# Four graph-attention layers on one core: alternating the step order to its end, and a new path for the last step

## The chip, the cores and the metric

The kernel runs on one core of a Trainium2 chip. TensorE (PE) does matrix products and transposes, VectorE (DVE), ScalarE (ACT) and GpSimd (POOL) do elementwise work, and SyncE (SP) issues the DMAs. Each engine works through its own instructions in program order; where one needs another's result it waits on a semaphore. The metric is device microseconds of one execution, the median of several; lower is better. All times below are microseconds unless marked ns.

## The reference

Sixteen independent batches of 1,024 nodes with 256 features go through four graph-attention layers. Each layer normalises its input, projects it, weighs every pair of neighbouring nodes and adds the weighted sum to its input:

```
h  = relu(layernorm(x))
q  = h @ W                      # heads: 4, 1, 4, 1
e  = leaky_relu(src(q)[i] + dst(q)[j])     # slope 0.2, 0.2, 0.2, 0.01
a  = softmax over j of e, where adj[i, j]
x += elu(a @ q)                 # relu in the last layer
```

`src` and `dst` are scalar products of a head's features with two halves of a vector. All is float32.

## The kernel before

**Steps.** A step is one layer of one batch: 64 steps. Layers 0 and 2 have four heads of 64 features (a *four-head* step), layers 1 and 3 one head of 256 (a *one-head* step). A batch's layers depend on each other, so four streams of batches are interleaved; `order_of_steps` (L635) lists the stream of each step in `turns`. The order alternates four-head and one-head steps, but its last nine entries end in four-head, four-head, one-head, one-head, one-head (steps 59 to 63: batches 14, 15, 13, 14, 15; layers 2, 2, 3, 3, 3). The last step, 63, is the last layer of batch 15; step 60 is the layer before it.

**The sum of a step.** The weight of a pair is written as a maximum of two products, so that for a head and a block of 128 nodes `jc` one VectorE instruction makes a tile of 128 x 1,024 unnormalised weights (`weights`, L386-391): the larger of `g` (a row spread over all partitions, in PSUM) and `rcol` (a column), times the 0/1 mask. There are 8 tiles per head, 32 in a four-head step. `aggregate` (L393) multiplies the tiles on TensorE with the projected features `whx` (L405), in eight groups a step, k = 0 to 7. A four-head group is half a head's nodes, a one-head group one block of 128 nodes over all 8 tiles. An extra column gives the sum of the weights, by which `finish` divides. ScalarE copies a group's sums from PSUM to `y` (L420). The tiles live in 18 buffers (`WBUFS`), so VectorE can be at most 18 tiles ahead of TensorE. Group sums, projections and transposes share four PSUM banks (`bank`).

**Finishing a step.** `finish(n)` (L426) returns pieces, each with the group of step n + 1 behind which it is emitted: the reciprocal of the sums (`divide`, L441, VectorE); `scaled` per half of the nodes: on VectorE min(y, 0) times the reciprocal (L451, layers with ELU and slack), on GpSimd y times the reciprocal (L452); the exponential on ScalarE (L458); and `add`: on VectorE max(exp - 1, y) (L464), on GpSimd the addition to x (L465). In the last layer, which has relu, `add` is one VectorE instruction (L467), and `store` writes the result out.

**Preparing a step.** `preparation(n)` (L229) returns 21 pieces in a fixed order: `stats` of two halves (four `bn_stats` each, L241), the combination of the moments, on VectorE for step 0 and else on GpSimd (L268-280; the power -0.5 is GpSimd's always, L274), `normalise` of two halves (ScalarE, L286), then per half two pieces of `transpose` and four of `project`, then `factors`, `rows`, the fetch of the heads, and an end mark. From step 2 on, the transpose goes through ScalarE (L295), a DMA transpose and ScalarE again (L303). Steps 0 and 1 transpose on TensorE (L317) and copy on ScalarE (L318). `project` is 4 matmuls a block (L328), a copy (L330), and at the end of a half two exponentials on ScalarE and a multiplication of `whx` on GpSimd (L340). `rows` transposes the factors (L352) and stores them in DRAM; `fetch` loads them spread over the partitions, and `broadcast` copies them to PSUM (`g`, ScalarE, L384). Only head 0 of step 0 makes `g` by eight TensorE transposes (L381).

**The order around it.** Everything is emitted by hand. Each kind of step has a table of 21 due times (`FOUR`, `ONE`, `NEXT`, `TIGHT` and others), counted in groups, eight to a step, from a start two steps ahead of its own. The main loop emits, for each group: tiles it still needs, the group's matmuls, pieces of `finish` that are due, heads, prepared pieces that are due, and tiles ahead. In the last step each group's division, relu, addition and store follow at once on VectorE and SP (L414-417).

Of the kernel before, what the change touches and what calls it, by code (L numbers as in the profile page):

```python
# [26 lines left out]
F32 = mybir.dt.float32  # L27
# [5 lines left out]
ALU = mybir.AluOpType  # L33
# [3 lines left out]
P = 128  # L37
# [3 lines left out]
WBUFS = 18  # L41
HBUFS = 6
# [4 lines left out]

FOUR = (-8, -8, -5, 0, 1, 0, 3, 5, 5, 5, 5, 1, 4, 5, 5, 5, 5, 6, 8, 8, 10)  # L50
SHORT = (-4, -4, -4, 0, 1, 0, 3, 5, 5, 5, 5, 1, 4, 5, 5, 5, 5, 6, 8, 8, 10)
NEXT = (-4, -4, -4, 1, 3, 2, 5, 8, 8, 8, 8, 4, 7, 8, 8, 8, 8, 9, 10, 10, 12)
# [1 line left out]
SOON = (0, 0, 0, 1, 2, 1, 3, 4, 4, 5, 5, 2, 5, 6, 6, 7, 7, 7, 8, 8, 10)  # L54
FIRST = (-4, -4, -4, -2, -0.9, -1, -1, -0.8, -0.8, -0.8, -0.8, 0, 0, 1, 1, 1, 1, 1, 2, 2, 4)
TIGHT = (4, 4, 4, 5, 6, 5, 7, 8, 8, 8, 8, 6, 8, 9, 9, 9, 9, 9, 10, 10, 12)
LATE = (0, 0, 0, 1, 2, 1, 3, 4, 4, 4, 4, 2, 4, 5, 5, 5, 5, 5, 6, 6, 8)


# [9 lines left out]
def kernel(ctx: ExitStack, tc: tile.TileContext, x, adj, ws, avs, out):  # L69
    nc = tc.nc  # L70
    B, N, F = x.shape
    C = N // P
# [156 lines left out]
    def preparation(n):  # L229
# [6 lines left out]
        def stats(half):  # L236
            if half == 0:
                st["bn"] = small.tile([P, C, 6], F32, name="bn")
            bn = st["bn"]
            for c in range(half * HALF, (half + 1) * HALF):  # L240
                nc.vector.bn_stats(bn[:, c, :], xs[b][:, c, :])  # L241
            q = slice(half * HALF, (half + 1) * HALF)
            if n == 0:
                if half == 1:
                    combine_end(slice(0, HALF), nc.vector)
                combine(q, nc.vector)
            elif H == 1:

                combine(q, nc.gpsimd)
                combine_end(q, nc.gpsimd)  # L250
# [55 lines left out]
                st["turned", half].rearrange("p s n i -> p (n i) s"), AF.Copy)  # L306

        def transpose(half, k):
            if n > 1:

                (merge if k else split)(half)
                return
            if k == 0:
                st["hT", half] = prep.tile([P, K, HALF * P], F32, name="rows", bufs=HBUFS)
            pt = bank(HALF, P)
            for q in range(HALF):
                nc.tensor.transpose(pt[:, q, :], st["xn", half][:, k, q, :], ident)  # L317
            nc.scalar.activation(st["hT", half][:, k, :], pt.rearrange("p q i -> p (q i)"),  # L318
                                 AF.Copy)
# [28 lines left out]

        def rows():

            pt = bank(P)[0:C * H]
            nc.tensor.transpose(pt, st["gcol"].rearrange("p c h -> p (c h)"), ident)  # L352
            gT = small.tile([C * H, P], F32, name="gT", bufs=2)
            nc.scalar.activation(gT, pt, AF.Copy)
            st["grow"] = dram.tile([H, C, P], F32, name="grow")
            nc.sync.dma_start(out=st["grow"].rearrange("h c i -> c h i"), in_=gT)
# [5 lines left out]


        out += [factors, rows, lambda: fetch_heads(n + 1), lambda: None]
        return [(at, piece) for at, piece in zip(agenda_of[n], out, strict=True)]

    def fetch(n, h):

        if n == 0 and h == 0:
            return  # L370
        gs = state[n]["gs", h] = work.tile([P, N], F32, name="gs", bufs=2)
        nc.sync.dma_start(out=gs, in_=state[n]["grow"][h].rearrange("c i -> (c i)")
                          .partition_broadcast(P))

    def broadcast(n, h):

        g = state[n]["g", h] = ps_g.tile([P, N], F32, name="g")
        if n == 0 and h == 0:

            for c in range(C):  # L380
                nc.tensor.transpose(g[:, c * P:(c + 1) * P],  # L381
                                    state[n]["gcol"][:, c, h:h + 1].to_broadcast([P, P]), ident)
            return
        nc.scalar.activation(g, state[n]["gs", h], AF.Copy)  # L384

    def weights(n, h, jc):  # L386

        w = state[n]["w", h, jc] = work.tile([P, N], F32, name="w", bufs=WBUFS)
        nc.vector.scalar_tensor_tensor(w, state[n]["g", h], state[n]["rcol"][:, jc, h:h + 1],  # L389
                                       masks[LAYERS[steps[n][1]][3]][:, jc, :],  # L390
                                       op0=ALU.max, op1=ALU.mult)

    def aggregate(n, h, i0, per):  # L393
        H = LAYERS[steps[n][1]][0]
# [31 lines left out]
    def finish(n):  # L426

        b, l = steps[n]
        H = LAYERS[l][0]
        D = F // H  # L430
        st = state[n]

        def views(half):
            s = slice(half * HALF, (half + 1) * HALF)
            return (xs[b][:, s, :].rearrange("p c (h d) -> p (c h) d", h=H),
                    st["y"][:, s, :, 0:D].rearrange("p c h d -> p (c h) d"),
                    st["r"][:, s, :].rearrange("p c h -> p (c h)"))

        def divide():
            st["r"] = small.tile([P, C, H], F32, name="r")  # L440
            nc.vector.reciprocal(st["r"], st["y"][:, :, :, D])  # L441

        def scaled(half):
            xh, yh, r = views(half)
            rb = r[:, :, None].to_broadcast([P, HALF * H, D])
            if l < L - 1:

                e = st["e", half] = prep.tile([P, HALF * H, D], F32, name="rows",
                                                    bufs=HBUFS)
                if H > 1 and slack(n):  # L450
                    nc.vector.scalar_tensor_tensor(e, yh, 0.0, rb, op0=ALU.min, op1=ALU.mult)  # L451
            nc.gpsimd.tensor_tensor(yh, yh, rb, op=ALU.mult)  # L452
            if l < L - 1 and not (H > 1 and slack(n)):
                nc.gpsimd.tensor_scalar(e, yh, 0.0, -3.0e38, op0=ALU.min, op1=ALU.max)  # L454

        def exponential(half):
            if l < L - 1:
                nc.scalar.activation(st["e", half], st["e", half], AF.Exp)  # L458

        def add(half):  # L460
            xh, yh, r = views(half)
            if l < L - 1:
                e = st["e", half]
                nc.vector.scalar_tensor_tensor(e, e, -1.0, yh, op0=ALU.add, op1=ALU.max)  # L464
                nc.gpsimd.tensor_add(xh, xh, e)  # L465
                return
            nc.vector.scalar_tensor_tensor(xh, yh, 0.0, xh, op0=ALU.max, op1=ALU.add)  # L467

        def store(half):
            nc.sync.dma_start(  # L470
                out=out[b].rearrange("(p c) f -> p c f", p=P)[:, half * HALF:(half + 1) * HALF],
                in_=xs[b][:, half * HALF:(half + 1) * HALF, :])
            if half == 1 and b + STREAMS < B:
                load(b + STREAMS)


        at = (0, 0, 0, 0, 1, 1, 1) if slack(n) and H > 1 else (0, 0, 1, 1, 2, 2, 3)
        return list(zip(at, (divide, lambda: scaled(0), lambda: scaled(1), lambda: exponential(0),
                             lambda: exponential(1), lambda: add(0), lambda: add(1)))) + (
                    [(4, lambda: store(0)), (4, lambda: store(1))] if l == L - 1 else [])  # L480
# [60 lines left out]
    for n, (b, l) in enumerate(steps):  # L541

        free = -99
        if b % STREAMS in last:
            over = last[b % STREAMS] + 1
            free = 8 * over + (8 if l == 0 else 2 if LAYERS[steps[over][1]][0] == 1 else 4)
        last[b % STREAMS] = n
        start = 8 * (n - 2)
        kind = ONE if LAYERS[l][0] == 1 else SOON if n < 3 else FOUR
        if kind is FOUR and free > start + kind[0]:  # L550
            kind = SHORT if slack(n - 2) else NEXT
        if kind is ONE and free > start + kind[0]:
            kind = TIGHT
        if free > start + kind[0]:
            kind = LATE
            start = max(free, agenda_of[-1][0] + 5, start - LATE[7])
        agenda_of.append([start + k for k in kind] if n > 1 else FIRST)
        if n > 2:


            assert agenda_of[n][7] >= 8 * (n - 2)
            assert agenda_of[n][3] >= agenda_of[n - 1][12]
    ending = []
    later = {}
    with tc.manual_schedule():
# [45 lines left out]
        for n in range(len(steps)):  # L611
            for k, (h, i0, per) in enumerate(groups(n)):
                while planned < len(steps) and min(
                        a[0] for a in agenda_of[planned:planned + 2]) <= 8 * n + k:
                    plan(planned)
                    planned += 1
                emit_tiles(place[n, h, C - 1] + 1, must=True)
                aggregate(n, h, i0, per)
                if i0 + per == C:
# [15 lines left out]
def order_of_steps(B, L):  # L635

    depth = B // STREAMS * L
    one = [[(k // L * STREAMS + s, k % L) for k in range(depth)] for s in range(STREAMS)]  # L640
    turns = [0, 1, 2, 0, 3, 1, 2] + [0, 3, 1, 0, 2, 1, 3, 2] * (depth // 2 - 2)
    turns += [0, 3, 1, 0, 2, 3, 1, 2, 3]
    return [one[s].pop(0) for s in turns]


# [22 lines left out]
```

## Time and profile before

| | |
|---|---|
| median of 3 runs | 2460.33 (2455.75 to 2462.64) |
| the profiled execution's own time | 2463.54 |
| its span, first to last instruction | 2461.8 |
| granted TensorE clock, mean | 0.994 |
| weights, VectorE L389 | 1,280 instructions, 1,273 ns mean, 1538.9 busy |
| sums, TensorE L405 | 36,864 instructions, 240 ns mean, 1899.5 busy |
| projections, TensorE L328 | 2,048 instructions, 393 ns mean, 489.3 busy |
| chain of waits by engine | PE 82%, ACT 6%, DVE 5%, DMA 4%, issue 2% |
| last matmul ends, us from the start | 2457.7 |

A row of the profile names the line, the engine, the operation, the tile written and the tiles read, then their shapes and a count. In the view in order of time the first two numbers are the start and the length of the row; several like instructions in a row are merged, and `[5.55 <-PE bank L405]` says that the engine had been idle for 5.55 us and what released it. Since a matmul's end is modelled and overlaps the next one, lengths of matmuls are best read from one row's start to the next row's start.

### The profile page before, as it was taken

Reading aid. Unit: us, or ns where it says so; the run is one execution under the profiler, and the core shown is the slowest. Engines: PE = TensorE matmul, PEld = TensorE weight load, DVE = VectorE, ACT = ScalarE, POOL = GpSimd, SP = SyncE. Lnnn points to the kernel's source line nnn. Section 1 sums busy time; section 2 is a strip of 40 time slices with the busy share of each in tenths; the row PEclk is TensorE's granted clock in tenths of the full one; section 3 lists DMA queues with packets and bytes.
Section 4 is the critical chain, followed back from the end, with each engine's and each line's share of the span. In section 5 each row is a group of like instructions: output and inputs, shape, how many; then the busy total and the mean of one; then the engine's idle time right before and its main releaser. Section 6 shows DMA issues by size and latency. Waiting matters only on the chain.

```text
span 2461.8 us, 86525 instructions
## 1 busy us (share of the span) xinstructions
PE 2396.4 (97%) x39104; PEld 2150.2 (87%) x39104; DVE 2041.2 (83%) x2138; ACT 1484.9 (60%) x2501; POOL 1074.7 (44%) x1366
## 2 busy tenths in 40 slices
PE   7989999999999999999999999999999999999899
PEld 5888798889898889898898888899988889888878
DVE  8988688888888988888988888988888888888963
ACT  5464676555666656765556765656665556765461
POOL 3344455543345454444343555453444344553341
PEclk9999999999999999999999999999999999999999
DMA  4322232233333322232433332323433422323221
GB/s 181 81 54 62 44 79 62 70 105 90 94 85 87 74 64 56 67 79 88 113 97 81 77 71 62 79 63 80 113 79 87 109 58 54 79 62 70 77 48 61
DMA packets 294761, 193.40 MB, mean 79 GB/s; under 512 B 264182, under 2 KB 266998, under 8 KB 292472
## 3 DMA queue, kind: packets, MB, share of 16 engines
q1 hardware_dynamic: 294382, 187.86, 30.2%
q8 instruction: 306, 5.01, 0.8%
q14 instruction: 63, 0.52, 0.1%
q10 hardware_dynamic: 10, 0.00, 0.0%
HBM read 105.39 MB, written 17.43 MB: 50 GB/s over the span
## 4 chain that ended last, share of the span: by engine, by line
PE 82%; ACT 6%; DVE 5%; DMA 4%; issue 2%; POOL 0%; SPq 0%; DVEq 0%; ACTq 0%
PE bank L405 64%; PE bank L328 18%; DVE w L389 4%; ACT rows L286 2%; DMA gs<-grow 2%; DMA grow<-gT 1%; ACT rows L295 1%; ACT g L384 1%; ACT rows L458 1%; ACT rows L303 1%; DVE bn L241 1%; ACT y L420 0%; DMA rows<-rows 0%; PE bank L352 0%; DVE rows L464 0%
## 5 line engine op out<-in xcount | busy, mean ns | idle before, releaser
L405 PE MATMUL bank<-whx,w 128*64 128x65 f32 x36864 | 1899.5, 240 | 26.4 <-DVE w L389 17.0
L405 PEld LDWEIGHTS bank<-whx,w 128*64 128x64 f32 x36864 | 1746.2, 144 | 186.5 <-issue 22.6
L389 DVE SCALAR_TENSOR_TENSOR w<-g,rcol,mask 128x1024 f32<-128x1024 f32 x1280 | 1538.9, 1273 | 206.1 <-PE bank L405 160.8
L340 POOL TENSOR_TENSOR whx<-whx 128x1024 f32<-128x1024 f32 x128 | 244.9, 1913 | 823.8 <-ACT whx L338 823.8
L420 ACT ACTIVATE y<-bank 128x260 f32<-128x260 f32 (+1 forms) x504 | 191.9, 381 | 567.1 <-PE bank L405 567.0
L328 PE MATMUL bank<-wx,rows 128*128 128x264 f32 (+1 forms) x2048 | 489.3, 393 | 16.0 <-ACT y L420 8.4
L328 PEld LDWEIGHTS bank<-wx,rows 128*128 128x128 f32 x2048 | 384.4, 192 | 92.5 <-ACT y L420 14.2
L452 POOL TENSOR_TENSOR y<-y,r 128x1024 f32<-128x1024 f32 x126 | 262.4, 2091 | 254.0 <-DVE rows L451 186.6
L330 ACT ACTIVATE whx<-bank 128x264 f32<-128x264 f32 (+1 forms) x512 | 193.6, 388 | 194.2 <-PE bank L328 193.5
L286 ACT ACTIVATE rows<-x,shift,rstd 128x256 f32<-128x256 f32 x512 | 264.5, 588 | 72.5 <-POOL shift L280 70.3
L465 POOL TENSOR_TENSOR x<-x,rows 128x1024 f32<-128x1024 f32 x96 | 227.1, 2365 | 181.6 <-DVE rows L464 181.6
L303 ACT ACTIVATE rows<-rows 128x2048 uint16<-128x2048 uint16 x124 | 265.9, 2144 | 21.5 <-DMA rows<-rows 21.5
L295 ACT ACTIVATE rows<-rows 128x2048 uint16<-128x2048 uint16 x124 | 236.9, 1911 | 3.9
L464 DVE SCALAR_TENSOR_TENSOR rows<-rows,y 128x1024 f32<-128x1024 f32 x96 | 187.9, 1957 | 49.1 <-ACT rows L458 43.7
L241 DVE BATCH_NORM_STATS2 bn<-x 128x6 f32<-128x256 f32 x512 | 175.5, 409 | 33.4 <-POOL x L465 30.0
L384 ACT ACTIVATE g<-gs 128x1024 f32<-128x1024 f32 x159 | 162.6, 1023 | 63.8 <-DMA gs<-grow 49.1
L274 POOL TENSOR_TENSOR rstd<-rstd,neghalf 128x4 f32<-128x4 f32 (+1 forms) x97 | 120.3, 1240 | 15.2 <-DVE shift L275 7.8
L458 ACT ACTIVATE rows<-rows 128x1024 f32<-128x1024 f32 x96 | 100.6, 1048 | 2.0 <-POOL rows L454 2.0
L441 DVE RECIPROCAL r<-y 128x32 f32<-128x32 f32 (+1 forms) x63 | 17.2, 274 | 96.3 <-ACT y L420 96.3
L451 DVE SCALAR_TENSOR_TENSOR rows<-y,r 128x1024 f32<-128x1024 f32 x58 | 70.1, 1250 | 1.1
L467 DVE SCALAR_TENSOR_TENSOR x<-y,x 128x1024 f32<-128x1024 f32 x30 | 36.5, 1215 | 8.9 <-POOL y L452 8.9
L338 ACT ACTIVATE whx<-whx,nbias 128x16 f32<-128x16 f32 (+1 forms) x128 | 40.3, 315 | 4.2
(67 smaller groups left out, 444.4 us busy)
## 6 DMA issues: line engine op xcount, KB each, us to landing
gs<-grow SPq DMA_DIRECT2D x159, 512.0 KB
x<-in_x SPq DMA_DIRECT2D x15, 1024.0 KB
out<-x SPq DMA_DIRECT2D x30, 512.0 KB
w<-in_adj SPq DMA_DIRECT2D x8, 512.0 KB
rows<-rows SPq DMA_TRANSPOSE x124
x<-in_x SPq DMA_DIRECT2D x2, 512.0 KB
wx<-in_L_gnn_W SPq DMA_DIRECT2D x8, 128.0 KB
out<-x SPq DMA_DIRECT2D x8, 128.0 KB
```

The lines of the kernel that those rows point to most:

```text
L241: nc.vector.bn_stats(bn[:, c, :], xs[b][:, c, :])
L286: nc.scalar.activation(xn[:, :, q, :], xs[b][:, c, :].rearrange("p (k i) -> p k i", k=K), AF.Relu, bias=st["shift"][:, c:c + 1], scale=st[ ...
L295: nc.scalar.activation(bits, xn.rearrange("p (n s) -> p s n", s=2), AF.Copy)
L303: nc.scalar.activation(st["hT", half].rearrange("p k i -> p (k i)").bitcast(U16).rearrange("p (n s) -> p n s", s=2), st["turned", half].re ...
L328: nc.tensor.matmul(pw, lhsT=st["hT", half][:, k, q * P:(q + 1) * P], rhs=wx[l][:, k, :], start=(k == 0), stop=(k == K - 1))
L330: nc.scalar.activation(st["whx"][:, c, :], pw, AF.Copy)
L340: nc.gpsimd.tensor_tensor(wh[:, :, :, 0:D], wh[:, :, :, 0:D], wh[:, :, :, D:D + 1].to_broadcast([P, HALF, H, D]), op=ALU.mult)
L389: nc.vector.scalar_tensor_tensor(w, state[n]["g", h], state[n]["rcol"][:, jc, h:h + 1], masks[LAYERS[steps[n][1]][3]][:, jc, :], op0=ALU.m ...
L405: nc.tensor.matmul(acc[o % P:o % P + cols, q, :], lhsT=st["w", h, jc][:, o:o + cols], rhs=st["whx"][:, jc, h * (D + 1):(h + 1) * (D + 1)], ...
L420: nc.scalar.activation(st["y"][:, i0:i0 + per, h, :], acc, AF.Copy)
L452: nc.gpsimd.tensor_tensor(yh, yh, rb, op=ALU.mult)
L465: nc.gpsimd.tensor_add(xh, xh, e)
```

## The change

The last nine entries of `turns` are replaced by one more round of the regular eight and a final stream 3. So steps 60 and 61 change places: 60 is batch 13's last layer (one head), 61 batch 15's third (four heads), then 62 and 63 as before. Only step 62 now stands between a step and the last one, which needs its result.

- The last step is prepared by a table of its own, `LAST`, which starts at step 62. Its three statistics pieces do nothing; `finish` of step 61 calls them through `state[-1]`.
- `finish` of step 61 consists of `begin` (emitted before step 62's first group), the exponential of half 1, and `end` (both behind group k = 1). All of it is VectorE's but the two exponentials. The statistics of step 63 stand between its pieces, combined on VectorE.
- Step 63's transposes go by TensorE, its `rows` are left out, and its `g` is made by eight TensorE transposes (`direct`).
- Step 63's weights are made in two halves of 512 columns, the first half of all eight tiles first.
- Step 60's `add` is two GpSimd instructions instead of one of VectorE.

```diff
+LAST = (0, 0, 0, 1, 3, 2.8, 2.8, 4, 4, 4, 4, 4, 4, 4, 4, 4, 4, 4, 5, 5, 5)
...
-            if n == 0:
+            if n == len(steps) - 1:
+                combine(q, nc.vector)
+            elif n == 0:
...
-            if n > 1:
+            if 1 < n < len(steps) - 1:
...
+            if n == len(steps) - 1:
+                return
             pt = bank(P)[0:C * H]
...
+        if n == len(steps) - 1:
+            st["stats"], st["combined"] = stats, lambda half: combine_end(
+                slice(half * HALF, (half + 1) * HALF), nc.vector)
+            out[0:3] = [lambda: None] * 3
...
+    def direct(n, h):
+
+        return h == 0 and n in (0, len(steps) - 1)
...
+        parts = 2 if n == len(steps) - 1 else 1
+        if parts > 1 and jc:
+            return
+        js = range(C) if parts > 1 else (jc,)
+        for j in js:
+            state[n]["w", h, j] = work.tile([P, N], F32, name="w", bufs=WBUFS)
+        for i in range(parts):
+            s = slice(i * N // parts, (i + 1) * N // parts)
+            for j in js:
+                nc.vector.scalar_tensor_tensor(
+                    state[n]["w", h, j][:, s], state[n]["g", h][:, s],
+                    state[n]["rcol"][:, j, h:h + 1],
+                    masks[LAYERS[steps[n][1]][3]][:, j, s], op0=ALU.max, op1=ALU.mult)
...
+            if n == len(steps) - 4:
+
+                nc.gpsimd.tensor_scalar(yh, yh, 0.0, 3.0e38, op0=ALU.max, op1=ALU.min)
+                nc.gpsimd.tensor_add(xh, xh, yh)
+                return
...
+        if n == len(steps) - 3:
+
+            def early(half):
+                xh, yh, r = views(half)
+                rb = r[:, :, None].to_broadcast([P, HALF * H, D])
+                e = st["e", half] = prep.tile([P, HALF * H, D], F32, name="rows", bufs=HBUFS)
+                nc.vector.scalar_tensor_tensor(e, yh, 0.0, rb, op0=ALU.min, op1=ALU.mult)
+                if half == 0:
+                    exponential(half)
+                nc.vector.tensor_tensor(yh, yh, rb, op=ALU.mult)
+
+            def late(half):
+                xh, yh, r = views(half)
+                e = st["e", half]
+                nc.vector.scalar_tensor_tensor(e, e, -1.0, yh, op0=ALU.add, op1=ALU.max)
+                nc.vector.tensor_add(xh, xh, e)
+
+            def begin():
+                divide()
+                early(0)
+                late(0)
+                state[-1]["stats"](0)
+                early(1)
+                state[-1]["combined"](0)
+
+            def end():
+                late(1)
+                state[-1]["stats"](1)
+                state[-1]["combined"](1)
+
+            return [(-1, begin), (1, lambda: exponential(1)), (1, end)]
...
+        if n == len(steps) - 1:
+            kind, start = LAST, 8 * (n - 1)
...
+                while ending and ending[0][0] < k:
+                    ending.pop(0)[1]()
                 emit_tiles(place[n, h, C - 1] + 1, must=True)
...
-    turns = [0, 1, 2, 0, 3, 1, 2] + [0, 3, 1, 0, 2, 1, 3, 2] * (depth // 2 - 2)
-    turns += [0, 3, 1, 0, 2, 3, 1, 2, 3]
+    turns = [0, 1, 2, 0, 3, 1, 2] + [0, 3, 1, 0, 2, 1, 3, 2] * (depth // 2 - 1) + [3]
```

More of the change, by code (lines that the diff above doesn't have):

```diff
@@ L364, in preparation @@
         out += [factors, rows, lambda: fetch_heads(n + 1), lambda: None]
+        if n == len(steps) - 1:
+            st["stats"], st["combined"] = stats, lambda half: combine_end(
+                slice(half * HALF, (half + 1) * HALF), nc.vector)
+            out[0:3] = [lambda: None] * 3
         return [(at, piece) for at, piece in zip(agenda_of[n], out, strict=True)]
+    def direct(n, h):
+        return h == 0 and n in (0, len(steps) - 1)
     def fetch(n, h):
-        if n == 0 and h == 0:
+        if direct(n, h):
             return
@@ L377, in broadcast @@
         g = state[n]["g", h] = ps_g.tile([P, N], F32, name="g")
-        if n == 0 and h == 0:
+        if direct(n, h):
             for c in range(C):
@@ L386, in weights @@
     def weights(n, h, jc):
[L388 to L391, printed above, removed]
+        parts = 2 if n == len(steps) - 1 else 1
[11 more added lines that the diff above has]
+                    masks[LAYERS[steps[n][1]][3]][:, j, s], op0=ALU.max, op1=ALU.mult)
     def aggregate(n, h, i0, per):
```

## The prediction

> **What bounds the kernel now.** I read the page's busy shares first, then the busy time by stretch, then TensorE alone in order of time.
>
> ```profile
> PE 2396.4 (97%) x39104; PEld 2150.2 (87%) x39104; DVE 2041.2 (83%) x2138; ACT 1484.9 (60%) x2501; POOL 1074.7 (44%) x1366
> ```
>
> TensorE is the bound: only its idle time can be won. The next view cuts the end of the run into two ordinary pairs of a four-head and a one-head step (55-56, 57-58) and everything after step 58. Columns: stretch, its length, busy us of PE, PEld, DVE, ACT, POOL, granted clock, DMA share, GB/s.
>
> ```profile
> 2117.80:2192.20 74.40, 74.01 (x1220) 66.45 (x1219) 63.02 (x65) 47.21 (x80) 36.62 (x44) 1.00 0.28 66
> 2192.20:2266.40 74.20, 73.55 (x1219) 66.19 (x1218) 62.27 (x58) 48.33 (x81) 30.93 (x24) 1.00 0.31 70
> 2266.40:2457.80 191.40, 179.26 (x2565) 158.92 (x2564) 124.54 (x140) 80.37 (x142) 64.35 (x84) 0.98 0.21 59
> ```
>
> Where the steps alternate, TensorE idles 0.4 to 0.7 us per pair. In the last five steps it idles 12.1 us, and the clock is not whole. The waits of TensorE in this last stretch name the cause (us, times, longest):
>
> ```profile
> PE bank L405 <- DVE w L389: 6.2, 9, 0.9
> PE bank L405 <- issue: 3.1, 4, 1.2
> PE bank L328 <- ACT rows L303: 2.6, 1, 2.6
> ```
>
> Steps 59 and 60 are both four-head, and 64 tiles of weights at 1.20 us make VectorE late. The rows of TensorE give the price of its work:
>
> ```profile
> 2323.47 11.42 PE L405 MATMUL bank<-whx,w 128*64 128x65 f32 x384
> ...
> 2361.25 5.75 PE L328 MATMUL bank<-wx,rows 128*128 128x258 f32 x16 [2.62 <-ACT rows L303]
> ...
> 2415.74 41.98 PE L405 MATMUL bank<-whx,w 128*128 128x257 f32 x192
> ```
>
> 384 matmuls to the next start take 11.35 us, so a four-head step (1,024) takes 30.3 us; 192 take 41.8, so a one-head step (128) takes 27.9; half a projection undisturbed is 3.67 us, a whole one 7.35. Work after step 58: 2 x 30.3 + 3 x 27.9 + 4 x 7.35 + 0.4 for four row transposes = 174.1 us. The stretch is 191.3, so **17.2 us are lost**: 12 as idle, 2.1 because the 16 matmuls above took 5.75 instead of 3.67, the rest in matmuls drawn out between late tiles.
>
> **The change, part by part.** Nothing differs before the preparations of steps 60 and 61, around 2230 us; I rebuild the time from 2266.4 on.
>
> *Steps 59 and 60* become one more ordinary pair: 74.3 us, the mean of the two above.
>
> *Step 61* (four-head, batch 15) keeps the one-head preparation for step 62, but loses the 7.35 us projection of a four-head step two ahead. Step 57 is its model: from 2192.2 to 2238.4, 46.2 us. Its 32 projection matmuls with a wait held 8.2 us (2222.53 to 2230.77). Step 61: 46.2 - 8.2 = 38.0. That projection was also VectorE's cover:
>
> ```profile
> 2206.53 7.24 DVE L389 SCALAR_TENSOR_TENSOR w<-g,rcol,mask 128x1024 f32<-128x1024 f32 x6 [5.55 <-PE bank L405]
> ...
> 2228.16 9.61 DVE L389 SCALAR_TENSOR_TENSOR w<-g,rcol,mask 128x1024 f32<-128x1024 f32 x8
> 2238.92 0.35 DVE L441 RECIPROCAL r<-y 128x32 f32<-128x32 f32 x1 [1.16 <-ACT y L420]
> 2239.31 2.36 DVE L451 SCALAR_TENSOR_TENSOR rows<-y,r 128x1024 f32<-128x1024 f32 x2
> ```
>
> At 2206.5 the first head's buffers come free; VectorE then has 22 tiles to make (14 of the step, 8 of the next), 22 x 1.20 = 26.5 us. TensorE needed 31.9 us to the end of step 57, and needs 23.7 without the projection. The 5 us of statistics and additions that lay between the tiles are gone too (statistics moved on, step 60's finish given to GpSimd, which is idle there), so VectorE ends its tiles **2.8 us after TensorE ends step 61**. TensorE just escapes: head 3's last tile is due at 16.8 and comes at 16.8, step 62's last is due at 26.7 and comes at 26.5. I add 0.1: 38.1 us.
>
> *Step 62* has to hide the whole hand-over of batch 15. I count from the end of step 61; TensorE's queue is four groups of 3.49 us, eight transposes (half 0), a group, projections 0-3, eight transposes (half 1), projections 4-7, a group, eight transposes for G, two groups. VectorE in order: free at 2.8; reciprocal 0.35; `early(0)` 1.18 and a product of 128x1024. Before has no such product on VectorE; a 128x256 one takes 0.42 (four of them 1.7), the two-input addition of L464, undisturbed, 1.21: I take 1.2, the like shape. `late(0)` 2 x 1.2 brings 8.0 (the exponential, 1.05 on ScalarE, lies beside the product). Statistics and their combination are seen at the start of the run:
>
> ```profile
> 5.17 1.41 DVE L241 BATCH_NORM_STATS2 bn<-x 128x6 f32<-128x256 f32 x4 [3.44 <-DMA x<-in_x]
> 6.61 0.17 DVE L268 TENSOR_TENSOR dev<-bn 128x4 f32<-128x4 f32 x1
> ...
> 7.56 0.16 DVE L275 TENSOR_TENSOR shift<-bn 128x4 f32<-128x4 f32 x1
> ```
>
> That is 1.4 + 1.0, so 10.4. The power is GpSimd's (1.04) while VectorE runs `early(1)`, which reads two SBUF operands. Here a rule speaks against the change: "SBUF — State Buffer" of the Trainium skill (section "SBUF: two separate sides") says VectorE and GpSimd share a port pair as an exclusive lock for the whole instruction, and that a VectorE operation with two SBUF inputs takes it. The trace has such a collision, a tiny GpSimd operation beside a VectorE addition (2294.16 to 2295.37):
>
> ```profile
> 2294.14 1.30 POOL L268 TENSOR_TENSOR dev<-bn 128x4 f32<-128x4 f32 x1
> ```
>
> The same operation alone takes 0.20. So by rule and row the power waits for `early(1)`'s first operation (to 11.6), ends at 12.7, the product at 13.9; without the lock the product ends at 12.8. I take the lock: +1.1 us. `combined(0)` 0.25, then four normalisations on ScalarE, 2.06: **16.2**, where TensorE's four groups ended at 13.95. Half 0's transposes end at 16.5. Half 1: `late(1)` 2.4, statistics 1.4, combination 1.0, power 1.05, end 0.25 from 14.1 gives 20.2; normalisation 22.3. TensorE meanwhile: group to 20.0, projections 0-2 to 22.7; projection 3 waits for a PSUM bank whose copy stands behind the normalisation on ScalarE, to 23.7; transposes 24.6; their copies stand behind four `whx` copies and two exponentials on ScalarE (26.0); projections 4-7 end at 29.2, a group 32.7, G 33.6, two groups **40.6**.
>
> Of this 37.9 is work (27.9 + 7.35 + 24 transposes); the transposes are priced by
>
> ```profile
> 31.77 1.04 PE L381 MATMUL g<-ident,gcol 128*128 128x128 f32 x8
> ```
>
> 0.88 to the next start, three times: 2.65 us. These are the real cost of going by TensorE, the bound engine; the rows' transpose saved is 0.1. The removed row stores, broadcast loads and DMA transposes of step 63 free only SP and queues that nothing waits for. Waits in step 62: 2.7 us.
>
> *Step 63*: 27.9. Its weights come in half tiles, each about 0.72 (an estimate between 0.48 for L415's 256 elements from PSUM and 1.20 for 1,024): eight from 33.6 end at 39.4, before 40.6; the other eight by 45.2, due at 54.5. The extra 2 us on VectorE are covered; were all 16 needed at once, step 63 would be late by 3.7.
>
> Sum: 74.3 + 38.1 + 40.6 + 27.9 = 180.9 against 191.3: **10.4 us less**. The tail after the last matmul (4.1 us) stays. Span 2461.8 - 10.4 = 2451.4; device time of the profiled execution 2463.54 - 10.4 = 2453.1. That execution lies 3.2 above the median of the runs, 2460.33; on the median the forecast is **2450**.
>
> **Bounds.** If VectorE is free as soon as step 61 ends, the first half stops waiting: 1.9 less. No lock: 1.1 less. The clock: by "TensorE: Matmul & The Clock Gate" of the Trainium skill (Part 1) half clock follows an idle window of about 3.4 us, so my gap of 1.7 us would cost nothing. The row is stricter: after a gap of only 2.62 us the matmuls at 2361 lost 2.1 us (granted clock 0.91 from 2362 to 2380). That gap ended a sparse stretch, mine follows dense work; I take nothing and keep 2.1 for the upper end.
>
> **Rivals.**
> - *Normalisation of half 0 waits for half 1 too* (they share tiles). It would start at 20.2 instead of 14.1, 6.1 us later: 2456. Against it: at the start of the run L286 began at 9.39, while the other half's combination was still running to 10.3.
> - *Step 61 starves.* The margin behind its tiles is nil. If the first release comes 5 us later, tiles, hand-over and TensorE all slip by 5: 2455. For it: the lost cover; against it: the 5.55 us in which VectorE idled before that release.
> - *Slower: the port.* If GpSimd holds the pair during the hand-over, each of eight two-input operations takes 2.7 instead of 1.2 (L464 took 2.78 at 2243.59 beside GpSimd's L452): 12 us, and two long gaps with a clock loss of 2.1 each: 16.2 later, 2466. It decides from 10.4 us, seven such collisions. For it: that row; against it: `early` and `late` leave GpSimd only the power.
> - *The change doesn't do what it says*: the stalls of 2293 to 2361 stay, because they come from the load of the end and not the order. 191.3 + 2.65 of transposes: 2463. Against it: the two pairs above, with the same load per pair.
>
> **Numbers.** Forecast 0.70, half 0 waiting 0.10, starving 0.09, port 0.08, no effect 0.03. A change within 0.3% (7.4 us) can't be told from none. The forecast's own range is 2446 to 2454; nearly all of it is beyond 0.3%, the two middle rivals reach it a quarter of the time; of port and no effect under half are slower by over 0.3%, and a little of all other cases is. Faster 0.71, same 0.22, slower 0.07. To leave out no more than 2 in 10 I take 2445 to 2458.
>
> **What would show it.** Right: after step 58 no L405 wait on L389 of more than a few tenths; step 60's addition on GpSimd; in step 62 a gap of 1 to 3 us before the eight L317 transposes and under 1.5 before projection 4; the first L389 of half a tile before the last two groups of step 62; last matmul near 2447. Wrong: L389 rows behind step 61's end by more than 4 us, the power above 2.5 us, or L286 of half 0 behind both statistics.

## The result and the profile after

The changed kernel takes **2448.66 us** (median of 11 runs, 2446.12 to 2456.29) against 2460.38 before (11 runs beside them); the ratio is 0.9957, 95% interval 0.9944 to 0.9969, that is 10.6 us less (7.6 to 13.8). The profiled execution took 2451.16 and its span is 2449.4, where before they were 2463.54 and 2461.8. Line numbers are higher after: L405 became L428, L328 L332, L389 L411.

First the busy time by stretch of the changed kernel, one line each for steps 59 and 60, step 61, step 62 and step 63 (stretch, length, busy us of PE, PEld, DVE, ACT, POOL, granted clock, DMA share, GB/s):

```profile
2264.90:2339.40 74.50, 73.72 (x1220) 66.35 (x1219) 61.15 (x57) 45.43 (x78) 26.25 (x30) 1.00 0.34 80
2339.40:2377.50 38.10, 38.10 (x1059) 36.20 (x1058) 32.52 (x29) 12.90 (x28) 19.10 (x8) 1.00 0.17 53
2377.50:2417.40 39.90, 38.66 (x187) 32.78 (x186) 24.21 (x48) 15.28 (x36) 6.82 (x4) 1.00 0.00 1
2417.40:2445.30 27.90, 27.90 (x129) 24.03 (x127) 15.44 (x31) 0.39 (x1) 3.74 (x2) 1.00 0.19 71
```

The last five steps take 180.4 us (2264.91 to 2445.32) where they took 191.3, so the stretch itself gives 10.9 us. The clock is whole in all four. The other 1.5 us between the two profiled executions lie ahead of step 59, in steps that the change does not touch, and are no gain of it. TensorE's waits in the same stretch (us, times, longest):

```profile
PE bank L332 <- ACT y L443: 0.8, 1, 0.8
PE bank L332 <- ACT rows L322: 0.8, 1, 0.8
PE bank L321 <- ACT rows L290: 0.5, 3, 0.2
```

The wait for the weights (L389 before) is gone, and so is the one for ScalarE's merge (L303). The 3.1 us that the profile before put down to issue are missing too; the last section comes back to them. The first line here lies in step 59 (at 2299.1); the other two, in step 62, are those of the hand-over. TensorE in order of time shows them in place, the one for the normalisations (L290) in the pieces into which the eight transposes of half 0 fall:

```profile
2391.52 0.33 PE L321 MATMUL bank<-ident,rows 128*128 128x128 f32 x1
2392.01 0.33 PE L321 MATMUL bank<-ident,rows 128*128 128x128 f32 x1 [0.16 <-ACT rows L290]
2392.50 0.33 PE L321 MATMUL bank<-ident,rows 128*128 128x128 f32 x1 [0.17 <-ACT rows L290]
2393.00 0.77 PE L321 MATMUL bank<-ident,rows 128*128 128x128 f32 x5 [0.16 <-ACT rows L290]
...
2400.62 1.03 PE L321 MATMUL bank<-ident,rows 128*128 128x128 f32 x8
2402.41 3.81 PE L332 MATMUL bank<-wx,rows 128*128 128x258 f32 x16 [0.75 <-ACT rows L322]
```

From 2391.5 each of the first transposes follows one normalisation, 0.49 us apart: the eight take 2.1 us instead of 0.9. Half 1's take 0.9, and then projection 4 waits 0.75 for their copies.

### The profile page after: what moved, and what is told of

It is laid out like the page before. It is cut to its first block, busy times and chain, and to the rows that moved or that the text cites. A ratio compares the mean times of both kernels' runs of the same rounds, so it can differ in the third digit from the quotient of the medians.

```text
span 2449.4 us, 86561 instructions
## 1 busy us (share of the span) xinstructions
PE 2393.3 (98%) x39127; PEld 2149.5 (88%) x39127; DVE 2048.9 (84%) x2168; ACT 1478.8 (60%) x2499; POOL 1069.9 (44%) x1346
## 4 chain that ended last, share of the span: by engine, by line
PE 80%; ACT 7%; DVE 6%; DMA 5%; issue 2%; POOL 0%; SPq 0%; DVEq 0%; ACTq 0%
PE bank L428 62%; PE bank L332 17%; DVE w L411 4%; DMA gs<-grow 2%; ACT rows L290 2%; DMA grow<-gT 2%; ACT rows L299 1%; ACT g L397 1%; ACT rows L481 1%; DVE bn L243 1%; ACT y L443 1%; ACT rows L307 0%; DMA rows<-rows 0%; DVE rows L487 0%; PE bank L358 0%
## 5 line engine op out<-in xcount | busy, mean ns | idle before, releaser
L428 PE MATMUL bank<-whx,w 128*64 128x65 f32 x36864 | 1896.7, 240 | 18.7 <-DVE w L411 9.8
L428 PEld LDWEIGHTS bank<-whx,w 128*64 128x64 f32 x36864 | 1745.6, 144 | 176.2 <-issue 21.7
L411 DVE SCALAR_TENSOR_TENSOR w<-g,rcol,mask 128x1024 f32<-128x1024 f32 (+1 forms) x1288 | 1539.8, 1268 | 195.9 <-PE bank L428 161.1
L332 PE MATMUL bank<-wx,rows 128*128 128x264 f32 (+1 forms) x2048 | 485.8, 391 | 14.7 <-ACT y L443 8.8
L332 PEld LDWEIGHTS bank<-wx,rows 128*128 128x128 f32 x2048 | 381.5, 191 | 90.3 <-ACT y L443 14.8
L290 ACT ACTIVATE rows<-x,shift,rstd 128x256 f32<-128x256 f32 x512 | 264.5, 588 | 66.6 <-POOL shift L284 61.4
L307 ACT ACTIVATE rows<-rows 128x2048 uint16<-128x2048 uint16 x122 | 261.7, 2145 | 20.6 <-DMA rows<-rows 20.6
L299 ACT ACTIVATE rows<-rows 128x2048 uint16<-128x2048 uint16 x122 | 233.1, 1911 | 3.9
L464 DVE RECIPROCAL r<-y 128x32 f32<-128x32 f32 (+1 forms) x63 | 17.3, 275 | 98.5 <-ACT y L443 98.5
L340 ACT ACTIVATE rcol<-whx,rbias 128x16 f32<-128x16 f32 (+1 forms) x128 | 39.9, 312 | 4.2
```

Source lines behind the costliest of these rows:

```text
L290: nc.scalar.activation(xn[:, :, q, :], xs[b][:, c, :].rearrange("p (k i) -> p k i", k=K), AF.Relu, bias=st["shift"][:, c:c + 1], scale=st[ ...
L299: nc.scalar.activation(bits, xn.rearrange("p (n s) -> p s n", s=2), AF.Copy)
L307: nc.scalar.activation(st["hT", half].rearrange("p k i -> p (k i)").bitcast(U16).rearrange("p (n s) -> p n s", s=2), st["turned", half].re ...
L332: nc.tensor.matmul(pw, lhsT=st["hT", half][:, k, q * P:(q + 1) * P], rhs=wx[l][:, k, :], start=(k == 0), stop=(k == K - 1))
L411: nc.vector.scalar_tensor_tensor(state[n]["w", h, j][:, s], state[n]["g", h][:, s], state[n]["rcol"][:, j, h:h + 1], masks[LAYERS[steps[n] ...
L428: nc.tensor.matmul(acc[o % P:o % P + cols, q, :], lhsT=st["w", h, jc][:, o:o + cols], rhs=st["whx"][:, jc, h * (D + 1):(h + 1) * (D + 1)], ...
```

## The experiments

Executions of the changed kernel scatter by some 10 us, and of the profiles some reach step 59 at 2262.6 and one at 2271.3, by way of the same instructions. So beside each ratio to the kernel before I give the *end length*: from step 61's first projection (L332) to the end of the last matmul, all in one profile. For the changed kernel it is 2339.39 to 2445.32, **105.9 us**; a second profile of it gave 106.2. The edits shift line numbers a little: the sums are L405, L407, L425 or L426 in some of the runs, the projections L328 or L330, the tiles L389, L391 or L409.

**1. The order alone.** The kernel before with the new `turns` and nothing else:

```diff
-    turns = [0, 1, 2, 0, 3, 1, 2] + [0, 3, 1, 0, 2, 1, 3, 2] * (depth // 2 - 2)
-    turns += [0, 3, 1, 0, 2, 3, 1, 2, 3]
+    turns = [0, 1, 2, 0, 3, 1, 2] + [0, 3, 1, 0, 2, 1, 3, 2] * (depth // 2 - 1) + [3]
```

> The kernel before with only the new order of steps; the last step keeps its ordinary preparation (statistics and combination on GpSimd, DMA transposes, rows through DRAM). Theory (order wins 17 us of lost time, the other edits keep the hand-over from eating it): steps 59 to 61 run as in the changed kernel, without waits for L389 above 0.3 us, but the serial chain of batch 15 (finish to 16, normalise to 25, DMA transposes and projections to 37, rows and fetch to 48, weights) makes step 63 start some 54 us after step 61 instead of 40: about 14 us later than the changed kernel, 2463, no gain over before. Rival (order alone does it, the rest is decoration): within 3 us of the changed kernel's 2449.

2470.77 us, ratio 1.0036 (1.0022 to 1.0049): slower than before. Steps 59 and 60 ran like the pair after (73.7 us), so the order does win its time; the end length was 127.5, that is 21.5 us more than with the whole change, where 14 had been expected. The chain that ended last, in order of time, tells why (start, us, what):

```profile
2381.92 2.77 POOL y L452
...
2387.69 5.58 POOL x L465 x2
...
2396.79 2.09 ACT rows L286 x4
...
2400.83 4.46 DMA rows<-rows
...
2405.32 2.15 ACT rows L303
...
2422.15 1.22 DMA grow<-gT
...
2423.39 3.65 DMA gs<-grow
...
2427.07 1.04 ACT g L384
```

With the finish and the statistics on GpSimd, the first normalisation (L286) starts 59.6 us after step 61 began, where the whole change starts it at 51.5. A DMA transpose holds up the chain for 4.5 us; the way of G through DRAM and back adds 5. In the ordinary steps all of that lies under other work. Here nothing is left to cover it. Step 61 also starved: TensorE waited for its tiles twice, by some 0.86 us, as in experiment 5.

**2. The ordinary finish.** The whole change, but step 61 finished partly on GpSimd and the last step's statistics as ordinary pieces:

```diff
-LAST = (0, 0, 0, 1, 3, 2.8, 2.8, 4, 4, 4, 4, 4, 4, 4, 4, 4, 4, 4, 5, 5, 5)
+LAST = (1, 1, 1, 1, 3, 2.8, 2.8, 4, 4, 4, 4, 4, 4, 4, 4, 4, 4, 4, 5, 5, 5)
...
-            if n == len(steps) - 1:
-                combine(q, nc.vector)
-            elif n == 0:
+            if n == 0:
...
-            out[0:3] = [lambda: None] * 3
...
-        if n == len(steps) - 3:
+        if False:
```

> The changed kernel, but step 61 is finished in the ordinary way (products and additions to x on GpSimd) and the last step's statistics are ordinary pieces behind group 1 with their combination on GpSimd. Theory: the first normalisation starts about 6 us later (from 13.4 to some 19.5 us after step 61), TensorE waits that much before the transposes of half 0, total about 6 us more than the changed kernel, 2455. Rival (a finish on GpSimd is hidden by the four groups): within 1 us of the changed kernel in the length of step 62.

2458.10, ratio 0.9987 (0.9981 to 0.9994); end length 113.8, **7.8 us more**. TensorE waits 5.7 us before the transposes, as the theory has it; the rest is clock. TensorE in order of time, then the granted clock (the third number from the right) in two stretches of 5 us:

```profile
2399.09 2.80 PE L319 MATMUL bank<-ident,rows 128*128 128x128 f32 x8 [5.69 <-ACT rows L288]
2401.68 5.23 PE L425 MATMUL bank<-whx,w 128*128 128x257 f32 x16
```

```profile
2395.00:2400.00 5.00, 0.90 (x2) 0.36 (x2) 1.34 (x4) 1.57 (x4) 3.95 (x16) 0.81 0.00 0
2400.00:2405.00 5.00, 4.97 (x15) 3.97 (x15) 0.00 (x0) 4.21 (x10) 1.65 (x4) 0.51 0.00 0
```

The clock falls to half during the gap of 5.69 us and stays there for nearly 6 us after it: the group takes 5.07 us to the next start instead of 3.49, and the eight transposes, paced by the normalisations in both kernels, 2.59 instead of 2.08. That is 2.1 us more on top of the gap, and 5.7 + 2.1 is the 7.8.

**3. The last step's transposes by DMA:**

```diff
-            if 1 < n < len(steps) - 1:
+            if n > 1:
```

> The changed kernel with the last step's transposes by ScalarE and DMA as in the ordinary steps. Theory: 1.8 us of TensorE work are saved, but ScalarE's split and merge (1.9 and 2.1 us a half) and some 2 to 4 us of DMA a half lie on the hand-over, and the second normalisation stands behind the first merge on ScalarE: step 62 longer by 7 to 12 us, about 2458. Rival (transposes on the bound engine are pure loss): shorter by up to 1.8 us.

2468.82, ratio 1.0026 (1.0017 to 1.0035); end length 123.2, 17.3 us more. The direction was right, the size not. TensorE:

```profile
2400.46 5.40 PE L332 MATMUL bank<-wx,rows 128*128 128x258 f32 x16 [6.88 <-ACT rows L307]
2415.27 6.51 PE L332 MATMUL bank<-wx,rows 128*128 128x258 f32 x16 [9.41 <-ACT rows L307]
```

Two gaps, one for each half: the second DMA transpose starts only once ScalarE, behind the first half's copies, has split its bits. And each gap is followed by projections at a reduced clock (0.62 granted from 2400 to 2405, 0.50 from 2415 to 2420): their rows are 5.4 and 6.5 us long instead of 3.7 and 3.8. The 16 transposes on the bound engine, 1.8 us, are the cheap way.

**4. The last step's G by DMA:**

```diff
-            if n == len(steps) - 1:
-                return
...
-        return h == 0 and n in (0, len(steps) - 1)
+        return h == 0 and n == 0
```

> The changed kernel with the last step's rows stored in DRAM and fetched back, no TensorE transposes for G. Theory: 0.8 us of TensorE saved, but store, fetch and copy (3.5 + 4.5 + 1.0 us) bring the first weights some 9 us behind group 5 instead of 1.5; the last two groups cover 7 us: TensorE waits 4 to 6 us at the start of step 63, total 3.5 to 5 us more, about 2453. Rival (the two groups cover it): 0.8 us less.

2451.98, ratio 0.9955 (0.9938 to 0.9972), in its median not to be told from the whole change; end length 108.2, **2.2 us more**, less than the 3.5 to 5 expected. TensorE waits for the first tile and then runs at the pace of the half tiles:

```profile
2417.90 29.54 PE L426 MATMUL bank<-whx,w 128*128 128x257 f32 x128 [1.27 <-DVE w L409]
```

Store and fetch took 1.2 + 4.5 us on the chain here, where I had counted 3.5 + 4.5.

**5. Step 60's addition on VectorE:**

```diff
-            if n == len(steps) - 4:
+            if False:
```

> The changed kernel with step 60's addition by VectorE (two instructions of 1.2 us) instead of GpSimd. Theory: VectorE's 22 tiles after the release take 2.4 us more, head 3 and step 62's tiles come late by as much, step 61 is longer by 2 to 2.4 us and step 62 about the same: 2 to 2.4 us more between the start of step 61 and that of step 63. Rival (VectorE has slack there): under 0.5 us more.

From step 61's start to step 63's: 80.5 us instead of 78.0, **2.5 more**; end length 108.4. TensorE's waits in steps 61 and 62 name the tiles:

```profile
PE bank L428 <- DVE w L411: 1.7, 2, 0.9
PE bank L332 <- ACT rows L322: 0.7, 1, 0.7
```

The clock adds to these waits (granted clock: the third number from the right):

```profile
2376.60:2380.20 3.60, 3.58 (x71) 3.58 (x73) 3.60 (x4) 0.00 (x0) 0.00 (x0) 0.55 0.02 5
```

At 0.55 these 3.6 us lose about 1.6; on the other hand the transposes of half 0 take 0.9 us here and not 2.1, as their normalisations are ready before TensorE is. Without the clock's loss the hand-over would have been late all the same: VectorE begins it (the reciprocal L464) 42.9 us after step 61's start, against 40.7 in the changed kernel. So VectorE has no slack left in step 61, and its two instructions of 1.2 us are paid nearly in full; that the sum lands on 2.5 is partly chance. (The median, 2454.37, ratio 0.9972, is clouded by the waits of step 59 told at the end.)

**6. Whole tiles in the last step:**

```diff
-        parts = 2 if n == len(steps) - 1 else 1
+        parts = 1
```

> The changed kernel with the last step's weights made as whole tiles. The prediction said 3.7 us if all were needed at once. Theory now: a one-head group takes its eight tiles one after the other, 0.44 us each, and whole tiles come every 1.2 us from the end of G's transposes on, the eighth at about 43.5 us after step 61 against 43.1 when it is due: under 1 us of waiting at the start of step 63. Rival (the halves are worth their 3.7 us): a wait of 3 us or more in the first group of step 63.

End length 106.5, 0.3 to 0.6 us more than the changed kernel's two profiles; median 2453.76, ratio 0.9962 (0.9951 to 0.9973). In step 63's first group TensorE shows one wait:

```profile
2427.18 25.02 PE L428 MATMUL bank<-whx,w 128*128 128x257 f32 x114 [0.16 <-DVE w L411]
```

From G's first transpose to the end it is 36.2 us, against 35.8 in both profiles of the changed kernel: the two parts are worth about 0.4 us here.

**7. The power before the early part of half 1:**

```diff
-                early(1)
                 state[-1]["combined"](0)
+                early(1)
```

> The changed kernel with the combination of half 0 ended before the early part of half 1 on VectorE, so that no VectorE operation with two SBUF operands runs beside the power on GpSimd. If the lock delays the power: it takes 1.0 us instead of 2.03, the first normalisation starts 1.2 to 1.5 us earlier, TensorE's wait before the transposes of half 0 falls from 1.9 to under 0.6 us; the second normalisation starts 1.0 to 1.3 us later, which the projections cover up to about 1.3 us; step 62 shorter by about 1 us. If the 2.03 us are something else: the power stays near 2 us and step 62 is no shorter.

End length 107.3, 1.3 us **more**; median 2457.21, ratio 0.9985 (0.9967 to 1.0002). GpSimd and ScalarE in order of time:

```profile
2389.65 1.04 POOL L278 TENSOR_TENSOR rstd<-rstd,neghalf 128x4 f32<-128x4 f32 x1 [20.61 <-DVE shift L279]
```

```profile
2392.25 1.06 ACT L481 ACTIVATE rows<-rows 128x1024 f32<-128x1024 f32 x1 [5.60 <-DVE rows L510]
2393.21 2.06 ACT L290 ACTIVATE rows<-x,shift,rstd 128x256 f32<-128x256 f32 x4
```

The first half of the expectation holds: without the two-operand operation beside it the power takes 1.04 us and not 2.03. The second does not: the shift was ready at 2391.1, but on ScalarE the exponential of half 1 is ahead of the normalisation, and that exponential had been moved back by the same edit. I had left ScalarE's order out. (The 1.9 us of the expectation were too high from the start: in the changed kernel the eight transposes take 1.2 us more than their work, which is what the first wait costs. The 1.7 in the next expectation stands for the same wait.)

**8. Other due times for the last step.** A first try:

```diff
-LAST = (0, 0, 0, 1, 3, 2.8, 2.8, 4, 4, 4, 4, 4, 4, 4, 4, 4, 4, 4, 5, 5, 5)
+LAST = (0, 0, 0, 1, 4.1, 4, 4, 5, 5, 5, 5, 4.9, 4.9, 5, 5, 5, 5, 5, 6, 6, 6)
```

> The changed kernel with other due times for the last step: transposes of half 0 behind group 4 instead of group 3, those of half 1 before all projections behind group 5, and G behind group 6. Theory (step 62's two waits, 1.7 and 0.8 us, are order on TensorE and not work): both go, step 62 takes 38 to 38.6 us instead of 40.0, and G with one group of cover still suffices because the half tiles come at 0.67 us each; total 1.5 to 2 us less than the changed kernel. Rival: the single covering group is too short and the wait returns at the start of step 63, no gain or a loss up to 2 us.

End length 107.5, 1.6 us more; median 2455.26, ratio 0.9971 (0.9962 to 0.9979). The first wait is gone, but there is a new one of 0.96 us before the transposes of half 1. ScalarE:

```profile
2400.20 0.39 ACT L443 ACTIVATE y<-bank 128x257 f32<-128x257 f32 x1 [2.83 <-PE bank L428]
2400.48 2.07 ACT L290 ACTIVATE rows<-x,shift,rstd 128x256 f32<-128x256 f32 x4
```

The normalisation's input was ready at 2397.9 (VectorE's L284 at 2397.69). A due time of 4.1 is emitted after group 5, hence behind that group's copy, for which ScalarE idled 2.8 us. So ScalarE's queue only moved the waiting to half 1. What makes the run slower than the changed kernel is the clock behind that wait:

```profile
2402.80:2405.80 3.00, 3.00 (x10) 2.60 (x10) 0.00 (x0) 1.32 (x3) 0.00 (x0) 0.50 0.00 0
```

The eight transposes behind the wait take 2.6 us, where the paced ones of the changed kernel take 2.1, and the 32 matmuls of the projections 8.1 us, where experiment 9 has 7.0: together 1.7, about the whole loss. None of this speaks about the order on TensorE, which the next run tells:

**9. Due times once more:**

```diff
-LAST = (0, 0, 0, 1, 4.1, 4, 4, 5, 5, 5, 5, 4.9, 4.9, 5, 5, 5, 5, 5, 6, 6, 6)
+LAST = (0, 0, 0, 1, 4, 3.9, 3.9, 5, 5, 5, 5, 4.9, 4.9, 5, 5, 5, 5, 5, 6, 6, 6)
```

> As the retimed kernel before it, but the normalisation of half 1 is emitted behind group 4, ahead of group 5's copy on ScalarE (in the first one it stood behind that copy, 2.6 us after its input was ready). Theory: normalisation of half 1 ends just as group 5 ends, no gap before the transposes of half 1 above 0.3 us, step 62 takes 38.0 to 38.6 us against 40.0 in the changed kernel, and step 63 starts without a wait; 1.5 to 2 us less in all. Rival (the one group behind G is too short a cover): 1 us or more of waiting at the start of step 63.

**2447.88** (5 runs, 2443.87 to 2448.70), ratio 0.9938 (0.9924 to 0.9951); end length **103.5, 2.4 us less** than the changed kernel. By stretch, step 62:

```profile
2377.30:2414.80 37.50, 37.50 (x188) 32.89 (x185) 20.72 (x43) 15.90 (x36) 6.83 (x4) 1.00 0.00 1
```

TensorE is busy through all of it, and nothing waits at step 63's start either; one group behind G is cover enough. That is a little more than the 1.5 to 2 us expected. What is firm is the end length: the median beats the changed kernel's beside it (experiment 10), but not clearly its first one, 2448.66.

**10. The changed kernel beside it**, without an edit:

> The changed kernel itself, beside the retimed one on the same chip. Expected: step 62 again 40.0 us within 0.2; steps 59 and 60 between 74.2 and 80 us (they took 74.5 in its profile, and 78 to 80 in three other runs of the same instructions, all in waits of step 59 that the profile puts down to issue), and a median 9 to 12 us under the kernel before.

2454.01 (6 runs, 2449.75 to 2456.95), ratio 0.9968 (0.9957 to 0.9980): 7.9 us under the kernel before, less than the 9 to 12 expected. Steps 61 to 63 are those of the first profile within 0.3 us, steps 59 and 60 took 73.7, a little under what was expected. Its profiled execution reached step 59 at 2271.3, where the one of experiment 9 was there at 2264.7. So of the 6.1 us between the two medians, the end lengths show 2.4 to 2.6 as the work of the due times; the rest I put down to the scatter ahead of step 59, which one profile of each cannot prove.

**11. TensorE's route in the old order.** The kernel before with the last step's transposes and G on TensorE, and nothing of the order:

```diff
-            if n > 1:
+            if 1 < n < len(steps) - 1:
...
+            if n == len(steps) - 1:
+                return
             pt = bank(P)[0:C * H]
...
-        if n == 0 and h == 0:
+        if h == 0 and n in (0, len(steps) - 1):
```

> The kernel before, in its old order, with only the last step's transposes and G by TensorE. Theory (24 transposes on the bound engine cost their 2.7 us and pay only where the hand-over is exposed): 2 to 3 us more than before, the late tiles of steps 59 to 61 unchanged. Rival (the DMA transposes and row fetches of the end cost time by themselves): faster than before by over 2 us.

2470.64, ratio 1.0037 (1.0024 to 1.0051): slower, by more than expected. Its last five steps take 199.5 us (from about 2265.0 to 2464.5) against 191.3 before, 8.2 more. TensorE's waits from step 59 on:

```profile
PE bank L407 <- DVE w L391: 5.1, 7, 0.9
...
PE bank L317 <- ACT rows L286: 2.9, 8, 1.0
```

The late tiles stay. To the 2.65 us of transposes come 2.9 in which TensorE stands right behind each normalisation, since the ordinary table puts both at the same group; a group after them took 5.2 instead of 3.6, at a granted clock of 0.50 from 2381.8 to 2384.8. That makes about 7 of the 8.2; the rest is not traced. This edit alone is a loss; it pays where the DMA route is exposed.

## Why the prediction was right

The forecast was 2450 on the median with 10.4 us less; measured were 2448.66 and 10.6 by the ratio. The stretch was forecast at 180.9 us and took 180.4. The agreement of the medians is partly luck: six more runs of the same kernel lay 7.9 us under the kernel before (experiment 10), and 1.5 us of the difference between the two profiled executions lie ahead of the change. The stretch is what carries the forecast. Step by step:

- *Steps 59 and 60* as an ordinary pair: forecast 74.3, measured 74.5. Experiment 1 shows that it is the order that does this.
- *Step 61*: forecast 38.1, measured 38.1, with VectorE free 2.6 us after TensorE (forecast 2.8). That the margin is nil was right: experiment 5 put 2.4 us on VectorE there, its hand-over began 2.25 later, and 2.5 were lost. The 22 tiles stand in one row, behind the release that was forecast:

```profile
2353.83 26.31 DVE L411 SCALAR_TENSOR_TENSOR w<-g,rcol,mask 128x1024 f32<-128x1024 f32 x22 [5.58 <-PE bank L428]
2380.06 0.34 DVE L464 RECIPROCAL r<-y 128x32 f32<-128x32 f32 x1
...
2384.29 1.22 DVE L519 TENSOR_TENSOR x<-x,rows 128x1024 f32<-128x1024 f32 x1
```

- *Step 62*: forecast 40.6, measured 39.9. The chain on VectorE ran as counted: half 0 was added at 8.0 (the end of L519 above; forecast 8.0), its combination was done at 10.6 (10.4). The product of 128x1024, which had no row before, took 1.23 (taken as 1.2).
- *The lock* is the term that was mis-sized: I gave it 1.1 us and it cost nothing. VectorE and GpSimd of the changed kernel:

```profile
2388.01 1.22 DVE L510 SCALAR_TENSOR_TENSOR rows<-y,r 128x1024 f32<-128x1024 f32 x1
2389.27 1.23 DVE L513 TENSOR_TENSOR y<-y,r 128x1024 f32<-128x1024 f32 x1
2390.41 0.16 DVE L283 TENSOR_TENSOR shift<-shift,rstd 128x4 f32<-128x4 f32 x1
```

```profile
2388.10 2.03 POOL L278 TENSOR_TENSOR rstd<-rstd,neghalf 128x4 f32<-128x4 f32 x1 [20.61 <-DVE shift L279]
```

  The power did wait for L510, as rule and row said: 2.03 us instead of 1.04, and experiment 7, without L510 beside it, confirms the cause. But I had made the product L513 wait for the power in turn, and it ran beside the power's second half. The power ended at 2390.13, before the product did, so the shift L283 stood at VectorE's own pace. It was ready at 13.3 us instead of my 14.15.
- *Waits in step 62*: forecast 2.7, measured 2.4, of which 1.2 among the transposes of half 0 and 0.75 before projection 4 can be read off. Experiment 9 shows that they were order and not work: step 62 takes 37.5 us without them, where I had put its work at 37.9. The 0.4 lie in the projection: I took 7.35, and between one-head groups both halves take 7.0 (experiment 9, 2400.03 to 2407.01).
- *Half tiles*: forecast as covered, with a loss of 3.7 us if all had been needed at once. Experiment 6 shows that price to be wrong as a measure of the edit: a group takes whole tiles one after another, and they cost about 0.4.
- *The clock*: I took nothing for a gap of 1.7 us. The wait came as small gaps between the transposes, none above 0.2, and the clock stayed at 1.00. This was not as safe as I thought: in experiments 8 and 11 a gap of 0.96 us with such gaps behind it was followed by 3 us at 0.50.

Of the rivals, the waiting half did not happen (L290 began at 2390.87, half 1's statistics at 2393.19), nor did the port: the eight two-operand operations took 1.22 to 1.23 us each, since GpSimd had nothing but the power. A starving of step 61 happened in experiments 1 and 5, though from step 60's additions on VectorE and not from a late release. "No effect" is ruled out, as TensorE no longer waits for the tiles (L411).

So the gain comes from the order, and the other edits are its condition: the order alone loses (experiment 1), and each hand-over edit taken back costs 7.8 (finish), 17.3 (transposes), 2.2 (G), 2.5 (addition) or about 0.4 us (parts). These prices overlap, and the first, second and fourth contain a loss of clock, so they do not add up to one sum.

## What to carry to other kernels

Where two kinds of step load different engines, alternating them to the end is worth what the trace shows as the wait in the unbalanced stretch, but the last dependent step loses its cover: count the chain from its predecessor through each engine's queue in program order and shorten it until it fits. A spare engine or a DMA that is free in the steady state can be the dearest choice in such a chain, and a transpose on the bound engine the cheapest. And due times are part of that chain: moving the last step's pieces by about a group gave 2.4 us, nearly a quarter of what the change gave, while one piece a place too late in ScalarE's queue turned that into a loss, most of it through the clock.

## What the runs showed of the hardware

- A long gap on TensorE is paid twice: the granted clock was 0.51 from 2400 to 2405, behind a gap of 5.69 us (experiment 2, 2.1 us lost). "TensorE: Matmul & The Clock Gate" of the Trainium skill (Part 1) names an idle window of about 3.4 us, after which the clock is halved, and this gap agrees. But the runs show half clock behind shorter gaps too: behind 2.62 us after sparse work in the kernel before (0.91 from 2362 to 2380), behind 2.81 us in experiments 5 and 6 (0.56 and 0.50 in the next 3 us), and in experiments 8 and 11 behind 0.96 us and three gaps of 0.17 between transposes (0.50 for 3 us). Nor does such a gap always cost: the clock stayed at 1.00 behind the same 2.81 us in experiment 7, behind the second group of transposes in experiment 11 (at 2387.96, again 0.96 and three of 0.17), and behind 1.27 us in experiment 4. What decides between them is open.
- A GpSimd operation of two SBUF reads blocked by VectorE is longer in its row, not later: 2.03 us instead of 1.04. Beside VectorE's tiles (L411), which read `g` from PSUM, the power takes 1.04 (at 2326.97). It doesn't hold up VectorE's next two-operand operation as long as its own row lasts: L513 began at 2389.27 and ran its 1.23 us, while the power's row went on to 2390.13. So the rule cited in the prediction, a lock for the whole instruction, held for the waiting power and did not show for L513.
- GpSimd's in-place maximum and minimum on `y` took 3.6 us, against 1.04 for the like operation from `y` into a buffer of its own (L454 before). What makes it slow was not tried; in step 61 nothing waited for it.

```profile
2355.71 3.64 POOL L492 TENSOR_SCALAR y<-y 128x1024 f32<-128x1024 f32 x1
2359.43 2.19 POOL L493 TENSOR_TENSOR x<-x,y 128x1024 f32<-128x1024 f32 x1
```

- In three profiles (experiments 5, 6, 7) step 59 held gaps of 0.56, 0.92 and 2.81 us that no semaphore explains, and steps 59 and 60 took 78.4 to 80.0 us instead of 73.5 to 74.6, though their instructions are the same. The gaps fall before the same matmuls each time. The three profiles come from one chip, but so does that of experiment 8, which has none. Both profiles in the old order hold 3.1 us of the same kind; of the eleven in the new order three hold 4.3, one 0.4 and seven none. So it is not settled whether the order removes them. The longest, in experiment 6:

```profile
2300.92 0.70 PE L428 MATMUL bank<-whx,w 128*64 128x65 f32 x9 [2.81 <-issue]
```

  Their cause stays open. They are a part of the scatter between executions, which is why the end lengths above carry the argument; the end lengths begin behind them.
